# Scores moved into the gate, two expert tiles behind the output products, a projection in 32-column tiles, and part of the reads' additions on ScalarE and GpSimd

## The chip, the cores and the metric

One core of a Trainium2 chip. The metric is the device time of one execution in microseconds (us); lower is better. A core has a matrix engine (TensorE, "PE" in the profile; "PEld" is its loading of weights), VectorE (DVE), ScalarE (ACT), GpSimd (POOL) and SyncE (SP, which here only issues DMAs). Each runs its own instructions in order and waits for others through semaphores. SBUF is the on-chip memory, PSUM the accumulators that TensorE writes.

## The reference, cut to what matters

A batch of 64 signals is cut into 157 frames of 512 samples (L = 157, D = 512). All numbers are fp32.

```python
h = dct(frames)                                   # 64 x 157 x 512
x = layernorm(h)
key, query = exp(i*pi*tanh(x @ Wk)), exp(i*pi*tanh(x @ Wq))   # 4 sets x 8 planes
V = x @ Wv + bv
total = sum over sets of weight * Re(cumsum(key * V) * conj(query))
pos   = the same with fixed position phases
g = sigmoid(x @ Wg + bg)
h = h + (g * total + (1 - g) * sigmoid(pw) * pos) / norm @ Wo + bo
y = layernorm(h)
e = argmax(softmax(mean_t(y) @ Wg2 + bg2))        # one of 16 experts for each signal
h = h + score_e * (y @ We[e] + be[e])
```

The causal sums are computed as attention: a matrix of scores between frames, masked, times V (the "reads").

## The kernel before, in words

The 64 signals go through in 16 groups of four (`GB`, `NG`). A group's 4 x 160 padded frames make five tiles of 128 rows, `n` = 0 to 3 and `TAIL`; 512 columns make four blocks `c` of 128. Groups overlap: while group g is in its attention, the experts of group g-1 and the embedding (the transform) of group g+1 are worked in between. For the middle groups the order is written out by hand, and each engine's queue follows the order of these calls:

- `project_and_values(g)` (L1085): `project` (L593) makes key and query phases, then the value products (seven products of a fast block scheme, `product`, L437, matmuls at L445), with the routing of group g-1 in between, which ends in fetching its four experts' weights.
- `gate(g)` (L1133): seven products (`gate_product`, L647, matmuls L655) in the order 1, 6, 2, 7, 5, 4, 3. Products 2, 4 and 3 accumulate onto the PSUM buffers of 1, 7 and 5, which stay held until then. VectorE adds each up into `gT`, ScalarE applies the tanh (L672). Between them lie embedding tiles of group g+1 (`embed`, L259, matmuls L270 and L272; their statistics on VectorE, L232) and `fold_twice` (L125) on VectorE, which prepares the next frames. Only in the last group (`not ahead`) does `scores` stand here, behind product 5.
- `experts_and_embedding(g)` (L1151): `scores(g)` (L674, 20 matmuls at L681, then two VectorE operations that make `att`), then expert tiles TAIL, 0 and 1 of group g-1 (`expert`, L960: 16 matmuls at L940, one addition on VectorE at L951, four or eight output DMAs on SyncE), and the scaling of the next residuals on ScalarE (`embed_res`, L319, L323).
- `attention(g)` (L1177): five bias additions on GpSimd (`add_bo`, L325, L327); four reads (`read`, L685, matmuls L697), with expert tile 2 behind the second; seven output products (L710, L445) with the tail's product (L250) behind the first; expert tile 3; GpSimd's sums for the next values (`value_sums`, L411, L414).

TensorE's 128 x 128 array is used in several tile shapes, which the profile prints as rows*columns: 128*128 for most products, 128*32 for scores and experts (four signals side by side in 32 columns each), 32*128 for the reads (four signals in 32 rows each), 128*64 for the projection.

PSUM is four buffers of two banks (`psum`, L91), taken in turn: a buffer is written again when all who read its last content are done. A read takes two buffers. Its result is used by VectorE, in four operations of 128 x 320 (L705): for each buffer it multiplies the gate by the first half of the result and then adds the second half, both out of PSUM.

The functions that the change touches, with the line numbers of the profile:

Of the kernel before, what the change touches and what calls it, by code (L numbers as in the profile page):

```python
# [14 lines left out]
F32 = mybir.dt.float32  # L15
I32 = mybir.dt.int32
AF = mybir.ActivationFunctionType
ALU = mybir.AluOpType
# [4 lines left out]
P = 128  # L23
# [4 lines left out]
LP = 160  # L28
Q = P // GB
NM = LP // Q  # L30
TAIL = NM - 1
SLOT = [0, 1, 3, 4, 2]
HT = P // 2
HN = HT + 2 * P
# [3 lines left out]
F = SETS * PLANES  # L38
# [15 lines left out]
def audio_tower(ctx: ExitStack, tc: tile.TileContext, a, out):  # L54
# [21 lines left out]
    nc = tc.nc  # L76
# [4 lines left out]
    p2 = pool("p2", 2)  # L81
# [9 lines left out]
    def psum():  # L91

        return ps_mm.tile([P, 2, 512], F32, tag="mm", name="mm")

    def bank():
        return psum()[:, 0, :]
# [3 lines left out]
    add = lambda *x: nc.vector.tensor_tensor(*x, ALU.add)  # L100

    def half(x, m):
        return x[:, :, HN * m : HN * (m + 1)]
# [73 lines left out]
    wkq = const.tile([P, C, 2 * F], F32, name="wkq", tag="wkq")  # L177
# [147 lines left out]
    def add_bo(g, n):  # L325
        r = S[g]["res"][n]
        nc.gpsimd.tensor_tensor(r, r, bo, ALU.add)  # L327
# [265 lines left out]
    def project(g):  # L593


        s = S[g]
        ps = psum()[:, 0, :]
        for c in range(C):
            for k in range(2):
                nc.tensor.matmul(  # L600
                    ps[2 * F * k : 2 * F * (k + 1), :HN],
                    wkq[:, c, :],
                    half(s["xT"], k)[:, c],
                    start=(c == 0),
                    stop=(c == C - 1),
                )
        s["u"] = u = p2.tile([P, 2, HN], F32, tag="even", name="u")
        nc.scalar.activation(u[:, 0], ps[:, :HN], AF.Tanh, bias=bkq)
# [65 lines left out]
    def scores(g):  # L674

        ps = bank()
        for n in range(NM):
            lo, hi = SEES[n]
            for i in range(GB):
                to = ps[Q * i : Q * (i + 1), START[n] : START[n] + hi - lo]  # L680
                nc.tensor.matmul(to, kf[:, SLOT[n], i], qf[:, lo // Q : hi // Q, i], start=True, stop=True)  # L681
        nc.vector.tensor_tensor(att[:, 0], ps[:, :NS], hmask, ALU.mult)
        nc.vector.tensor_tensor(att[:, 1], att[:, 0], share, ALU.add)

    def read(g, c):  # L685

        s = S[g]
        parts = [psum(), psum()]
        banks = [ps[:, b, : 2 * LP] for ps in parts for b in range(2)]

        for n in (3, 0, 1, 2, TAIL):
            for i in range(GB):
                q = slice(Q * i, Q * (i + 1))
                lo, hi = SEES[n]
                to = banks[i].rearrange("p (s t) -> p s t", s=2)[:, :, lo:hi]
                by = att[q, :, START[n] : START[n] + hi - lo]
                nc.tensor.matmul(  # L697
                    to, s["v", n][q, c * P : (c + 1) * P], by, start=(n == 3), stop=(n == TAIL)
                )
        for k, ps in enumerate(parts):  # L700
            of = slice(2 * k, 2 * k + 2)
            r = ps[:, :, : 2 * LP].rearrange("p b (s n t) -> p b s n t", s=2, n=NM)
            th = s["gT"][:, c].rearrange("p (n b t) -> p b n t", n=NM, b=GB)[:, of]
            for n, op in enumerate((ALU.mult, ALU.add)):
                nc.vector.tensor_tensor(th, r[:, :, n], th, op)  # L705

    def output_product(g, i):

# [152 lines left out]
    t = lambda name, shape, dt=F32: p2.tile(shape, dt, tag=name, name=name)  # L861
# [40 lines left out]
    def pick_gate(g):  # L902

        s = S[g]
        logit, top, rev = (s.pop(k) for k in ("logit", "top", "rev"))
        nc.vector.tensor_tensor(logit, logit, over(top), ALU.subtract)
        nc.scalar.activation(logit, logit, AF.Exp)
        expf = t("expf", [P, 1])
        for i in range(GB):
            q = slice(Q * i, Q * (i + 1))  # L910
            nc.vector.tensor_scalar(expf[q], rev[q, i : i + 1], -1.0, float(E), ALU.mult, ALU.add)
        s["expi"] = expi = t("expi", [P, 1], I32)
        nc.vector.tensor_copy(expi, expf)
        den = t("den", [P, 1])
        for i in range(GB):
            q = slice(Q * i, Q * (i + 1))
            nc.vector.tensor_reduce(den[q], logit[q, i], AX.X, ALU.add)
        s["gate"] = gate = t("gate", [P, 1])
        nc.vector.reciprocal(gate, den)
# [16 lines left out]
    def expert_chunk(g, n, c, ps):  # L936

        s = S[g]
        for i in range(GB):
            nc.tensor.matmul(  # L940
                ps[Q * i : Q * (i + 1), :],
                s["x2T"][:, c, i, Q * n : Q * (n + 1)],
                s["ws"][i][:, c, :],
                start=(c == 0),
                stop=(c == C - 1),
            )

    def expert_out(g, n, ps):
        s = S[g]
        o, at = s["res"][n], Q * BLOCK[n]  # L950
        nc.vector.scalar_tensor_tensor(o, ps, s["gate"], o, ALU.mult, ALU.add)  # L951
        for i in range(GB):

            for lo, hi in ((0, Q),) if n < TAIL else ((0, Q // 2), (Q // 2, LT)):
                queue = nc.sync if g + 1 < NG or i % 2 == 0 else nc.scalar
                if g + 2 == NG and n in ORDER[1:4]:
                    queue = nc.gpsimd
                queue.dma_start(out=out[GB * g + i, at + lo : at + hi, :], in_=o[Q * i + lo : Q * i + hi, :])

    def expert(g, n, between=lambda c: None):  # L960
        ps = psum()
        for c in range(C):
            between(c)
            expert_chunk(g, n, c, ps[:, 0, :])
        between(C)
        expert_out(g, n, ps[:, 0, :])
# [166 lines left out]
    def gate(g):  # L1133
        ahead = g + 1 < NG
        for i in (1, 6, 2, 7, 5, 4, 3):
            gate_product(g, i)
            if i == 1:
                pick_gate(g - 1)
                bias(g - 1)
                fold_once(g + 1, 1)  # L1140
                add_bv(g, 0, slice(H, D))
                add_bv(g, 1)
            if i == 5:
                if not ahead:
                    scores(g)
                fold_twice(g + 1, 1)
            for n in {6: (0,), 2: (1,), 3: (2, 3, TAIL)}.get(i, ()) if ahead else ():
                embed(g + 1, n)
                embed_statistics(g + 1, n)

    def experts_and_embedding(g):  # L1151

        new = g + 1
        scores(g)
        embed_deviations(new)
        add_bias(g - 1, TAIL)
        add_bias(g - 1, 0)
        expert(g - 1, TAIL)
        load_half(g + 2, 0)
        load_half(g + 2, 1)  # L1160
        for n in (1, 2, 3):
            add_bias(g - 1, n)
        for n in range(NM):
            embed_res(new, n)
        expert(g - 1, 0)
        keep_deviations(new)
        expert(g - 1, 1)
        spread_deviations(new)
# [8 lines left out]
    def attention(g):  # L1177
        ahead = g + 1 < NG
        if ahead and g > 0:
            for n in range(NM):  # L1180
                add_bo(g + 1, n)
        if g == 0:
            for _ in weight_sums(wg, t_g, nc.gpsimd):
                pass
        for c in range(C):
            read(g, c)
            if c == 1 and ahead and g > 0:
                expert(g - 1, 2)
        S[g]["blocks"] = halves(S[g]["gT"])
        made = token_sums(g, tail=False)  # L1190
        if g == 0:
            for n in (0, 1):
                add_bo(1, n)
        for i in (1, 2, 6, 7, 5, 4, 3):
            output_product(g, i)
            if i == 1:
                for _ in range(4 if g else 3):
                    next(made)
                if g == 0:
                    scale_all(1)  # L1200
                output_tail(g)
                statistics2(g, (TAIL,))
            elif i == 6:
                normal2(g, TAIL)
            elif i == 7 and g == 0:
                next(made)
            elif i == 5 and g == 0:
                value_sums(1)
            elif i == 5 and ahead:
                scale_all(g + 1)  # L1210
        if 0 < g and ahead:
            expert(g - 1, 3)
        for of in ((0, 1),) if ahead else ((0,), (1,)):
            statistics2(g, of)
        if 0 < g and ahead:
            value_sums(g + 1)
        normal2(g, 2)
        normal2(g, 3)
        if not ahead:
            normal2(g, 0)  # L1220
# [15 lines left out]
    g = NG - 1  # L1236
# [158 lines left out]
```

## Time and profile before

| | |
|---|---|
| time, median of 3 runs | 1320.94 us (1320.14 to 1323.14) |
| profiled execution, its own time | 1321.05 us |
| its span in the trace | 1319.1 us |
| granted TensorE clock | 0.999 |
| TensorE busy in L940 (experts, 2400 records) | 276.2 us |
| TensorE busy in L697 (reads, 2048 + 512 records) | 114.6 + 23.9 us |
| TensorE busy in L600 (projection, 256 records) | 38.0 us |
| TensorE busy in L681 (scores, 640 records) | 16.6 us |
| VectorE in L705 (additions of the reads, 256) | 116.8 us, 488 ns each |
| GpSimd in L327 (bias additions, 80) | 95.1 + 20.3 us |

A line of a group in the profile reads: line, engine, operation, output<-inputs, shapes, count, busy time and mean length of one. The ends of matmuls are modelled and overlap the next, so times on TensorE are best taken from one start to the next. A timeline is a list in order of time; equal neighbours are merged, and what stands in brackets is the idle time ahead of an instruction and who ended it.

### The profile page before, as it was taken

What the parts mean: (1) busy time and instruction counts of PE and PEld (TensorE: products, weight loads), DVE (VectorE), ACT (ScalarE), POOL (GpSimd) and SP (SyncE); (2) the same over time, 40 slices, a digit from 0 to 9 for tenths busy, and PEclk for the clock granted to TensorE, in tenths of its full rate; (3) what the DMA queues carried; (4) which work ended last, traced back from release to release, by engine and by line L of the source; (5) the groups of instructions that cost most, each with busy time, mean ns of one, the idle gap of its engine ahead of it and who ended that gap; (6) DMA issues with size and microseconds to landing.
All of it is one profiled execution on the core that took longest, in us unless ns stands there. A gap on an engine that the chain in (4) does not pass through costs nothing.

```text
span 1319.1 us, 25336 instructions
## 1 busy us (share of the span) xinstructions
PE 1312.0 (99%) x9784; PEld 921.5 (70%) x9784; DVE 1065.2 (81%) x2116; ACT 405.8 (31%) x708; POOL 551.0 (42%) x706
## 2 busy tenths in 40 slices
PE   9999999999999999999999999999999999999998
PEld 6677677677676767677676766776767676776762
DVE  6888798788878878788887978888788787887683
ACT  2524233141422314234141331414233042341310
POOL 2356345243533426245153452436334262452424
PEclk9999999999999999999999999999999999999999
DMA  7015224152331425314252241523314252141506
GB/s 238 1 51 176 83 56 182 37 176 83 113 135 42 161 81 175 92 49 152 75 176 83 68 171 36 176 82 121 126 51 156 79 184 83 48 152 35 178 8 207
DMA packets 60574, 144.40 MB, mean 109 GB/s; under 512 B 14136, under 2 KB 31432, under 8 KB 52520
## 3 DMA queue, kind: packets, MB, share of 16 engines
q1 hardware_dynamic: 45620, 62.68, 16.8%
q0 software_dynamic: 14336, 79.47, 16.3%
q8 instruction: 78, 1.28, 0.4%
q10 hardware_dynamic: 500, 0.64, 0.2%
q14 instruction: 40, 0.33, 0.1%
HBM read 102.47 MB, written 20.62 MB: 93 GB/s over the span
## 4 chain that ended last, share of the span: by engine, by line
PE 97%; issue 1%; DMA 1%; POOL 1%; DVE 0%; POOLq 0%
PE mm L445 29%; PE mm L940 20%; PE mm L655 17%; PE mm L250 9%; PE mm L697 9%; PE mm L600 3%; PE mm L270 3%; PE mm L272 3%; PE mm L636 1%; PE mm L681 1%; PE mm L201 1%; DMA t_v<-in_we,rows 1%; PE mm L219 0%; PE mm L191 0%; PE mm L835 0%
## 5 line engine op out<-in xcount | busy, mean ns | idle before, releaser
L940 PE MATMUL mm<-we,x2T 128*32 128x512 f32 x2400 | 276.2, 593 | 0.0
L940 PEld LDWEIGHTS mm<-we,x2T 128*32 128x32 f32 x2400 | 130.2, 109 | 111.0 <-issue 65.2
L237 POOL TENSOR_SCALAR rstd<-mv 128x2 f32<-128x2 f32 (+1 forms) x50 | 11.7, 235 | 396.9 <-DVE mv L233 396.9
L705 DVE TENSOR_TENSOR gT<-mm,gT 128x320 f32<-128x320 f32 x256 | 116.8, 488 | 37.7 <-PE mm L697 33.1
L697 PEld LDWEIGHTS mm<-att,v 32*128 32x128 f32 x2048 | 94.9, 185 | 34.0 <-issue 21.0
L697 PE MATMUL mm<-att,v 32*128 32x320 f32 (+3 forms) x2048 | 114.6, 358 | 0.0
L327 POOL TENSOR_TENSOR res<-res,bo 128x512 f32<-128x512 f32 x64 | 95.1, 1514 | 13.1 <-ACT res L323 13.0
L771 ACT ACTIVATE x<-res,shift,rstd 128x512 f32<-128x512 f32 x61 | 46.4, 808 | 162.2 <-POOL shift L244 161.4
L232 DVE BATCH_NORM_STATS2 st<-res 128x6 f32<-128x512 f32 x128 | 87.7, 685 | 2.8
L445 PE MATMUL mm<-t_o,sum 128*128 128x256 f32 x384 | 85.5, 379 | 0.0
L951 DVE SCALAR_TENSOR_TENSOR res<-mm,gate,res 128x512 f32<-128x512 f32 x64 | 47.9, 748 | 44.9 <-PE mm L940 42.9
L515 POOL TENSOR_TENSOR v<-v,bv 128x512 f32<-128x512 f32 (+1 forms) x45 | 72.7, 1634 | 26.6 <-ACT v L464 26.6
L237 POOL TENSOR_SCALAR dev<-mv 128x5 f32<-128x5 f32 (+1 forms) x20 | 4.9, 244 | 183.2 <-DVE mv L233 182.6
L445 PE MATMUL mm<-t_v,sum 128*128 128x256 f32 x360 | 80.1, 379 | 0.0
L445 PEld LDWEIGHTS mm<-t_o,sum 128*128 128x128 f32 x384 | 73.0, 190 | 9.9
L672 ACT ACTIVATE gT<-gT,hbg 128x320 f32<-128x320 f32 x90 | 45.6, 554 | 96.4 <-DVE gT L100 96.4
L445 PEld LDWEIGHTS mm<-t_v,sum 128*128 128x128 f32 x360 | 68.4, 190 | 9.3
L894 POOL DMA_INDIRECT we<-in_we,rows x60 | 60.3, 1005 | 34.4 <-DVE rows L890 20.3
L323 ACT ACTIVATE res<-res,shift,more 128x512 f32<-128x512 f32 x64 | 46.9, 803 | 89.2 <-POOL more L313 89.2
L716 ACT COPY u<-mm 128x512 f32<-128x512 f32 x16 | 9.4, 585 | 202.9 <-PE mm L445 202.9
L250 PE MATMUL mm<-wv,xT 128*128 128x512 f32 x160 | 71.8, 592 | 0.0
L655 PE MATMUL mm<-xT,wg 128*128 128x320 f32 x240 | 69.5, 432 | 0.0
(218 smaller groups left out, 2834.5 us busy)
## 6 DMA issues: line engine op xcount, KB each, us to landing
xT<-in_frames SPq DMA_DIRECT2D x32, 640.0 KB
out<-res SPq DMA_DIRECT2D x236, 64.0 KB
x2T<-turned SPq DMA_DIRECT2D x150, 80.0 KB
x2T<-turned POOLq DMA_DIRECT2D x90, 80.0 KB
scale<-row SPq DMA_DIRECT2D x15, 320.0 KB
out<-res_t SPq DMA_DIRECT2D x62, 32.0 KB
out<-res_t SPq DMA_DIRECT2D x62, 26.0 KB
wg<-in_wg SPq DMA_DIRECT2D x1, 1024.0 KB
```

The costliest lines, as they stand in the source:

```text
L232: nc.vector.bn_stats(st, h)
L250: nc.tensor.matmul(ps, tile_of(x[:, c], n), w[:, c, :], start=(c == 0), stop=(c == C - 1))
L323: nc.scalar.activation(s["res"][n], s["res"][n], AF.Identity, bias=shift, scale=more)
L327: nc.gpsimd.tensor_tensor(r, r, bo, ALU.add)
L445: nc.tensor.matmul(ps[:, b, :], lhs[:, c, P * b : P * (b + 1)], w[:, c, :], start=(first and c == 0), stop=(c == 1), skip_group_check=not ...
L515: nc.gpsimd.tensor_tensor(v, v, by, ALU.add)
L655: nc.tensor.matmul(ps[:, o, :HN], w[:, c, o * P : (o + 1) * P], rhs[:, c], start=(first and c == 0), stop=(c == 1), skip_group_check=not f ...
L697: nc.tensor.matmul(to, s["v", n][q, c * P : (c + 1) * P], by, start=(n == 3), stop=(n == TAIL))
L705: nc.vector.tensor_tensor(th, r[:, :, n], th, op)
L894: nc.gpsimd.indirect_dma_start(out=ws[b][:, n * k : n * (k + 1)], out_offset=None, in_=of, in_offset=bass.IndirectOffsetOnAxis(ap=rows[:, ...
L940: nc.tensor.matmul(ps[Q * i : Q * (i + 1), :], s["x2T"][:, c, i, Q * n : Q * (n + 1)], s["ws"][i][:, c, :], start=(c == 0), stop=(c == C - 1),
L951: nc.vector.scalar_tensor_tensor(o, ps, s["gate"], o, ALU.mult, ALU.add)
```

## The change

- `project`: for each of the four blocks and each half of the frames, one matmul of 64 columns (keys and queries together) becomes two of 32 columns, into the same PSUM rows.
- `scores(g)` is called in `gate`, behind product 5, for every group, and no longer at the start of `experts_and_embedding`.
- `attention`: expert tile 2 moves from behind the second read to behind the output products, in front of tile 3. Two bias additions stay ahead of the reads; that of tile 2 comes behind read 0, those of tile 3 and TAIL behind read 1.
- `read`: in groups 1 to 15, for blocks 0 and 1, the second half is copied out of PSUM by ScalarE into a buffer `rest` (of two), and GpSimd adds it to the gate; VectorE only multiplies. Blocks 2 and 3 stay as they were.

```diff
         for c in range(C):
-            for k in range(2):
+            for k, n in np.ndindex(2, 2):
                 nc.tensor.matmul(
-                    ps[2 * F * k : 2 * F * (k + 1), :HN],
-                    wkq[:, c, :],
+                    ps[2 * F * k + F * n : 2 * F * k + F * (n + 1), :HN],
+                    wkq[:, c, F * n : F * (n + 1)],
                     half(s["xT"], k)[:, c],
...
-            for n, op in enumerate((ALU.mult, ALU.add)):
-                nc.vector.tensor_tensor(th, r[:, :, n], th, op)
+            nc.vector.tensor_tensor(th, r[:, :, 0], th, ALU.mult)
+            if g > 0 and c in (0, 1):
+                rest = p2.tile([P, 2, LP], F32, tag="u", name="rest").rearrange("p b (n t) -> p b n t", n=NM)
+                nc.scalar.copy(rest, r[:, :, 1])
+                nc.gpsimd.tensor_tensor(th, th, rest, ALU.add)
+            else:
+                add(th, r[:, :, 1], th)
...
             if i == 5:
-                if not ahead:
-                    scores(g)
+                scores(g)
                 fold_twice(g + 1, 1)
...
         new = g + 1
-        scores(g)
         embed_deviations(new)
...
         if ahead and g > 0:
-            for n in range(NM):
+            for n in (0, 1):
                 add_bo(g + 1, n)
...
             read(g, c)
-            if c == 1 and ahead and g > 0:
-                expert(g - 1, 2)
+            if ahead and g > 0:
+                for n in ((2,), (3, TAIL), (), ())[c]:
+                    add_bo(g + 1, n)
...
         if 0 < g and ahead:
+            expert(g - 1, 2)
             expert(g - 1, 3)
```

## The prediction

> **What bounds the kernel now.** I read the page first: its busy shares and the chain of work that ended last.
>
> ```profile
> PE 1312.0 (99%) x9784; PEld 921.5 (70%) x9784; DVE 1065.2 (81%) x2116; ACT 405.8 (31%) x708; POOL 551.0 (42%) x706
> ...
> PE 97%; issue 1%; DMA 1%; POOL 1%; DVE 0%; POOLq 0%
> ```
>
> TensorE is busy from end to end, so other engines matter only if they stop it. What remains is time lost *inside* its busy time, and for that I took its timeline through one middle group (group 3; the groups repeat every 79.95 us). Columns: start, length, line, shape, number of records (a matmul of the source leaves two).
>
> ```profile
> 285.69 2.32 PE L655 MATMUL mm<-xT,t_g 128*128 128x320 f32 x8
> 287.85 2.32 PE L655 MATMUL mm<-sum,wg 128*128 128x320 f32 x8
> ...
> 291.79 0.61 PE L270 MATMUL mm<-dct_e,xT 128*128 128x128 f32 x4
> 292.23 0.61 PE L272 MATMUL mm<-trig_o,xT 128*128 128x129 f32 x4
> 292.77 1.03 PE L681 MATMUL mm<-qf,kf 128*32 128x128 f32 x40
> 293.66 11.16 PE L940 MATMUL mm<-we,x2T 128*32 128x512 f32 x96
> 304.75 1.80 PE L697 MATMUL mm<-att,v 32*128 32x320 f32 x32
> ...
> 308.39 3.64 PE L940 MATMUL mm<-we,x2T 128*32 128x512 f32 x32
> 311.96 1.80 PE L697 MATMUL mm<-att,v 32*128 32x320 f32 x32
> ...
> 315.60 1.99 PE L445 MATMUL mm<-wo,gT 128*128 128x256 f32 x8
> 317.43 3.60 PE L250 MATMUL mm<-wo,gT 128*128 128x512 f32 x8
> ```
>
> Lengths overlap, so time is taken from start to start. One expert tile alone (L940, 308.39 to 311.96) takes 3.57; eight full records of the same 512 columns (L250, 317.43 to the next start at 320.87) take 3.44. So four 32-column tiles do run side by side, and 0.13 is lost at the two seams where the tile shape changes. But three expert tiles in a row, straight behind the scores (293.66 to 304.75), take 11.09 and not 3 x 3.44 + 0.13 = 10.45: **0.64 us is lost there, in every middle group** (11.09 to 11.16 in all fourteen). The semaphore instructions of L940 in the two stretches point to the cause:
>
> ```profile
> L940 PEldq EVENT_SEMAPHORE  x12: 51/51/51, 293.2 to 298.0; - x12
> ```
> ```profile
> L940 PEldq EVENT_SEMAPHORE  x1: 51/51/51, 307.8 to 307.8; - x1
> ```
>
> The three tiles carry 12 waits, the single tile one, and the first ten of the 12 begin at 293.23, only 0.43 before the first expert matmul, and run 0.105 apart: four ahead of the first column tile's weights, two ahead of each other's. They come due as the matmuls should start, so the four column tiles start 0.23 apart (3 x 0.23 = 0.69) and stay staggered to the end. The 40 short score matmuls leave TensorE's queue little time to run ahead; before the projection a wait of L600 passes 2.67 before its matmul.
>
> The last view is the last group, which has its scores inside the gate and four reads in a row already:
>
> ```profile
> 1243.58 1.03 PE L681 MATMUL mm<-qf,kf 128*32 128x128 f32 x40
> 1244.54 2.42 PE L655 MATMUL mm<-xT,t_g 128*128 128x320 f32 x8
> 1246.80 2.32 PE L655 MATMUL mm<-sum,wg 128*128 128x320 f32 x8
> ...
> 1252.58 2.03 PE L697 MATMUL mm<-att,v 32*128 32x320 f32 x26
> ```
>
> **The change, part by part** (us; groups 1 to 14 unless said).
>
> *Scores into the gate.* Now: 292.77 to 304.75 = 11.98 for scores and three experts. After: the scores cost 0.96 (1243.58 to 1244.54), the seam into them 0.09 (the last embedding half takes 0.54, its like 0.45; that seam stays, now into the experts), and the seam out 0.10 (the product behind them 2.26, against 2.16 in the middle): 1.15. The experts then stand behind the embedding, whose 24 records of 0.11 give the queue 2 us to run ahead (its wait for the last embedding tile passes at 289.48, 2.3 before use), and ten waits need 10 x 0.105 = 1.05. I take the experts at 10.45: 1.15 + 10.45 = 11.60, **-0.38**. If the stagger stays it is 1.15 + 11.09 = 12.24, **+0.26**.
>
> The Trainium skill, "TensorEngine Tiling (Array Packing)", Key Properties, says that a change of tiling mode drains TensorE, while tiles of one mode run independently. The seams agree: 0.09 to 0.13. By that rule alone the scores stand best where they are, next to experts of their own shape, and moving them only adds two drains; the +0.26 is that result. The row of 11.09 speaks for the other.
>
> On VectorE the two operations that make att (0.63 + 0.66, now at 297.43) come in front of the folding at 286.70. The folding then ends at 290.05 instead of 288.6, product 4 is added by 290.9, product 3 by 292.2; the embedding tiles that take their PSUM buffers start at 292.06 and 292.95. Nothing, by 0.7; if that cover goes, each 0.1 beyond it costs 1.4 in all. VectorE's embedding statistics end 1.2 later, but without att behind them, so the bias additions start as before.
>
> *Third expert tile out of the reads.* Now four reads and one expert: 304.75 to 315.60 = 10.85. Two reads without the seam out take 3.53 (71.53 to 75.06, first group), two without the seam in 3.64 - 0.05 = 3.59: 7.12. The expert joined to the fourth is 3.44 more. 10.56, **-0.29**. Its VectorE addition (L951, 0.75) and four output DMAs move along. SyncE is idle there from 317.2 to 335.8. VectorE waits for the tile's end with the statistics of tiles 0 and 1 queued behind it; they already wait for the fourth tile, whose distance to the projection is unchanged. The scale for the next xT is issued at 314.99, DMA traffic ends by 319, and its reader (L363, 328.58) comes 3.4 earlier: cover of 6.
>
> *Projection in 32-column tiles.* Expert and projection now: 331.32 to 337.19 = 5.87. After: same shape as the expert, so no seam between them: 3.44 + 0.03 (seam in) + eight rounds of 320 columns at 2.16 (285.69 to 287.85) + 0.10 (seam out) = 5.73, **-0.14** (groups 2 to 15). Twice as many instructions: the weight loads (110 ns, four overlapping, 54 ns apart by L940's 130.2 us for 2400) need 0.22 per round of 0.27. Bounds: -0.25 (no seam out either) to 0.
>
> *Additions of the reads.* Without relief, four reads in a row are limited by VectorE: in the last group the second pair takes 1252.58 to 1256.94 = 4.36 against 3.59, a loss of 0.77. With reads 0 and 1 relieved, VectorE has two multiplications (0.47 apart) per read there, ScalarE a copy of 320 columns (0.43, between 0.27 for 129 and 0.585 for 512), and ScalarE has nothing else from 304.07 to 317.6. Counted from the first read: read 0 ends at 2.0, its second multiplication and copy by 3.0, the buffers are wanted at 3.5; read 1 the same by 4.9, wanted at 5.3. So **0**, and -0.77 once in group 15.
>
> GpSimd is the narrow place. The first output product needs the halves of reads 0 and 1, its second weight load at 7.12 + 0.43 - 0.19 = 7.36. GpSimd has no addition of this shape in the trace; contiguous ones take 0.45 for 128 columns, 1.27 for 512, 1.54 for 640, so 320 should be 0.87; bounds 0.69 (512's time per column, less half its start-up) and 1.29 (0.87 x 1.88/1.27, the slowest bias addition over the usual). In order: two additions from 2.6 (1.74), the bias addition of tile 2 (1.27), two more (1.74): done at 7.35. **0**, with no margin; each 0.1 in one addition costs 0.4 a group, 5.6 in all. I take 0.87 because the bias additions at 304.86 to 308.6 run beside the same multiplications (L705) at 1.27; the slow ones (1.88, 1.72) stand beside L934, which reads two SBUF operands. The other two bias additions follow at 7.4 to 9.9; GpSimd now idles 14.2 before its next work there.
>
> The Trainium skill, "GPSIMD Engine Reference", Engine selection, advises VectorE for elementwise work, GpSimd being some 2x slower with two inputs. By that an addition is 2 x 0.488 (L705) = 0.98, the product starts 0.43 late, and the sum is 6 us worse. The rows (1.27 for 512) speak for 0.87.
>
> **Sum.** 14 x (-0.38 - 0.29 - 0.14) = -11.3, and -0.77: -12.1. The profiled execution took 1321.05 (span 1319.1), 0.1 from the median of 1320.94, so **1309.0**.
>
> **Rivals.**
> 1. *GpSimd ends late and TensorE waits at the first output product.* Slower from 0.86 a group, that is from 1.09 an addition. At 1.29: 4 x 0.42 = 1.7 x 14 = 23.5, so 1332.5; with the bias addition slow too, 1341. For: no margin, strided operands. Against: the 1.27 beside L705. 0.11. A smaller lateness (up to 0.7) gives 1312 to 1318.5: 0.12.
> 2. *The stagger stays*, or waits are the same behind the embedding: 14 x (0.26 - 0.29 - 0.14) - 0.8 = -3.2: 1318.0. For: the ten waits are still there, behind an embedding tile that itself waits for a buffer. Against: 2 us of running ahead. 0.09. (The Trainium skill's drain rule, cited above from "TensorEngine Tiling (Array Packing)", gives the same time.)
> 3. *The relief does not reach the reads* (ScalarE's copies wait for their two buffers, which GpSimd's additions free): 0.77 x 15 = 11.5 lost: 1320.5. Against: 0.4 of margin. 0.06.
> 4. The forecast: 0.62, 1306 to 1312.
>
> 0.2% (2.6 us) is about what a measurement of this kernel can tell. Faster: 0.62 + 0.12 + over half of rival 2 = 0.80; slower 0.11; within 0.2%, the rest: 0.09. The range is 1306 (projection at -0.25, and some) to 1318.5, leaving out rivals 1 in full and 3.
>
> **What would show it.** The experts behind the embedding take 10.45 from start to read, with the waits of L940 earlier than the last embedding tile; four reads take 7.1 and the next L445 starts without idle; the GpSimd additions show 0.87; L600 shows 128*32, starting 6.9 after the third expert tile. If L445 behind the reads waits for GpSimd, or L940 still takes 11.09 for three, the forecast is wrong by that row.

## The result, and the profile after

The changed kernel takes 1311.06 us (median of 4 runs, 1311.03 to 1312.64) against 1320.97 (1320.14 to 1323.14): a ratio of 0.9928, 95% interval 0.9916 to 0.9939, so 0.7% faster. The forecast was 1309.0, in a range of 1306.0 to 1318.5. The profiled execution took 1311.08, its span 1309.1.

TensorE's timeline of the changed kernel in the same group 3 (start, length, line, shape, records), from the moved scores to the first output product; new line numbers: the experts are L945, their additions L956, the routing's matmul L840:

```profile
284.40 1.03 PE L681 MATMUL mm<-qf,kf 128*32 128x128 f32 x40
285.36 2.42 PE L655 MATMUL mm<-xT,t_g 128*128 128x320 f32 x8
...
292.55 10.51 PE L945 MATMUL mm<-we,x2T 128*32 128x512 f32 x96
302.98 1.80 PE L697 MATMUL mm<-att,v 32*128 32x320 f32 x32
...
310.11 2.08 PE L445 MATMUL mm<-wo,gT 128*128 128x256 f32 x8
312.03 3.60 PE L250 MATMUL mm<-wo,gT 128*128 128x512 f32 x8
```

Three experts from start to read: 302.98 - 292.55 = 10.43, where they took 11.09. The four reads: 310.11 - 302.98 = 7.13. Both are the forecast's (10.45 and 7.12). The scores cost 0.96, and 0.10 in the product behind them (285.36 to 287.62 = 2.26 instead of 2.16), as in the last group before. The waits of the experts are still there, but early: the first at 290.46, 2.1 before the first expert matmul, and nine of the eleven have passed by 291.5.

```profile
L945 PEldq EVENT_SEMAPHORE  x11: 51/51/51, 290.5 to 296.9; - x11
```

The next stretch, from the two joined expert tiles to the value products:

```profile
246.56 7.08 PE L945 MATMUL mm<-we,x2T 128*32 128x512 f32 x64
253.45 2.34 PE L600 MATMUL mm<-xT,wkq 128*32 128x320 f32 x32
255.72 1.99 PE L445 MATMUL mm<-wv,xT 128*128 128x256 f32 x8
...
269.62 0.33 PE L840 MATMUL mm<-own,mean 128*128 128x64 f32 x2
269.92 1.99 PE L445 MATMUL mm<-wv,sum 128*128 128x256 f32 x8
```

Two experts and the projection take 255.72 - 246.56 = 9.16 (forecast 3.44 + 5.73 = 9.17). But two places have become longer. From L840 to value product 3 it is 0.30, where it was 0.17. The kernel before, in the same group (L835 is there the routing's matmul; of product 3 the view shows three records):

```profile
271.14 0.33 PE L835 MATMUL mm<-own,mean 128*128 128x64 f32 x2
271.31 0.92 PE L445 MATMUL mm<-wv,sum 128*128 128x256 f32 x3
```

And the first output product takes 1.92 up to the tail's product (310.11 to 312.03), where it took 1.83. With 0.13 and 0.09 lost, a middle group takes 79.36 from projection to projection instead of 79.95; the fourteen distances together are 8.6 shorter. The last group's four reads take 7.19 instead of 7.89, less the 0.1 behind L840: 0.6. That is 9.2 of the 10.0 by which the span fell. Of the rest some 0.6 lies in the last experts, where TensorE waits for weights from DMA, and 0.1 ahead of the first projection; neither was followed.

The 0.09 has a plain releaser (an instruction that the waiting one needed) in the list of waits (total us, times, longest), and GpSimd's timeline shows when it ended:

```profile
PEld mm L445 <- POOL gT L708: 3.2, 14, 0.2
```
```profile
306.02 1.69 POOL L708 TENSOR_TENSOR gT<-gT,rest 128x320 f32<-128x320 f32 x2 [1.42 <-ACT rest L707]
307.65 1.28 POOL L327 TENSOR_TENSOR res<-res,bo 128x512 f32<-128x512 f32 x1
308.88 1.70 POOL L708 TENSOR_TENSOR gT<-gT,rest 128x320 f32<-128x320 f32 x2
```

The last of GpSimd's additions ends at 310.58, 7.60 after the first read; the forecast had 7.35.

The 0.13 shows no releaser by name. VectorE's timeline gives one by time:

```profile
253.70 0.75 DVE L956 SCALAR_TENSOR_TENSOR res<-mm,gate,res 128x512 f32<-128x512 f32 x1 [2.68 <-PE mm L945]
...
259.69 1.88 DVE L99 TENSOR_TENSOR sum<-sum,xT 128x640 f32<-128x640 f32 x1 [1.44 <-POOL sum L411]
...
269.05 0.81 DVE L99 TENSOR_TENSOR sum<-xT,sum 128x640 f32<-128x640 f32 x1
```

The last row writes the sum that value product 3 loads as weights. It ends at 269.86, and the load starts at 269.92. Read backwards: VectorE has no gap of note from 259.69 on; there it had waited 1.44 for GpSimd's first sums (L411), which stand in GpSimd's queue behind the statistics of tiles 0 and 1, which follow the addition of the *fourth expert tile* (253.70). In the kernel before the same sum ended at 270.44 + 0.82 = 271.26, and product 3 started at 271.31: no wait shows, but no time to spare either. So my theory was: from the end of that tile two ways lead to product 3, TensorE's (projection and six products) and this one, and the shorter projection has only made TensorE wait for the other. The rival: the projection's gain is real, and the time went elsewhere.

### The profile page after: what moved, and what is told of

The parts are those of the page before. It is cut to its first block, busy times and chain, and to the rows that moved or that the text cites. A ratio compares the mean times of both kernels' runs of the same rounds, so it can differ in the third digit from the quotient of the medians.

```text
span 1309.1 us, 25859 instructions
## 1 busy us (share of the span) xinstructions
PE 1302.9 (100%) x10040; PEld 863.6 (66%) x10040; DVE 1026.9 (78%) x2056; ACT 432.5 (33%) x768; POOL 603.1 (46%) x766
## 4 chain that ended last, share of the span: by engine, by line
PE 98%; POOL 1%; DMA 1%; issue 0%; DVE 0%; POOLq 0%
PE mm L445 29%; PE mm L945 20%; PE mm L655 18%; PE mm L250 9%; PE mm L697 9%; PE mm L270 3%; PE mm L272 3%; PE mm L600 3%; PE mm L636 1%; PE mm L681 1%; PE mm L201 1%; DMA t_v<-in_we,rows 1%; PE mm L219 0%; PE mm L191 0%; PE mm L840 0%
## 5 line engine op out<-in xcount | busy, mean ns | idle before, releaser
L945 PE MATMUL mm<-we,x2T 128*32 128x512 f32 x2400 | 264.1, 593 | 0.0
L945 PEld LDWEIGHTS mm<-we,x2T 128*32 128x32 f32 x2400 | 74.8, 110 | 167.3 <-issue 165.5
L956 DVE SCALAR_TENSOR_TENSOR res<-mm,gate,res 128x512 f32<-128x512 f32 x64 | 47.9, 749 | 73.1 <-PE mm L945 73.1
L237 POOL TENSOR_SCALAR dev<-mv 128x5 f32<-128x5 f32 (+1 forms) x20 | 10.5, 525 | 196.8 <-DVE mv L233 196.2
L704 DVE TENSOR_TENSOR gT<-mm,gT 128x320 f32<-128x320 f32 x128 | 59.5, 484 | 42.6 <-PE mm L697 42.5
L100 DVE TENSOR_TENSOR gT<-mm,gT 128x320 f32<-128x320 f32 (+3 forms) x128 | 71.4, 567 | 23.9 <-PE mm L655 20.9
L327 POOL TENSOR_TENSOR res<-res,bo 128x512 f32<-128x512 f32 x64 | 81.6, 1288 | 13.1 <-ACT res L323 13.0
L445 PE MATMUL mm<-t_o,sum 128*128 128x256 f32 x384 | 85.5, 379 | 0.0
L445 PE MATMUL mm<-t_v,sum 128*128 128x256 f32 x360 | 80.1, 379 | 0.0
L445 PEld LDWEIGHTS mm<-t_o,sum 128*128 128x128 f32 x384 | 73.0, 190 | 9.9
L445 PEld LDWEIGHTS mm<-t_v,sum 128*128 128x128 f32 x360 | 68.4, 190 | 9.3
```

Of the source, the lines that this page charges most:

```text
L445: nc.tensor.matmul(ps[:, b, :], lhs[:, c, P * b : P * (b + 1)], w[:, c, :], start=(first and c == 0), stop=(c == 1), skip_group_check=not ...
L704: nc.vector.tensor_tensor(th, r[:, :, 0], th, ALU.mult)
L945: nc.tensor.matmul(ps[Q * i : Q * (i + 1), :], s["x2T"][:, c, i, Q * n : Q * (n + 1)], s["ws"][i][:, c, :], start=(c == 0), stop=(c == C - 1),
```

## The experiments

All edits are to the changed kernel, unless said. The kernel before ran beside each set: 1320.8 to 1321.4.

**The projection back in 64 columns.**

```diff
-            for k, n in np.ndindex(2, 2):
+            for k in range(2):
                 nc.tensor.matmul(
-                    ps[2 * F * k + F * n : 2 * F * k + F * (n + 1), :HN],
-                    wkq[:, c, F * n : F * (n + 1)],
+                    ps[2 * F * k : 2 * F * (k + 1), :HN],
+                    wkq[:, c, :],
```

> The changed kernel with the projection back in 64-column tiles, all else kept. Theory A: the shorter projection (0.14 us a group) only brings TensorE sooner to value product 3, which waits for VectorE's sum (L99), a chain that starts at the end of the fourth expert tile and not at the projection. Then the time stays at 1311.1 (1310.6 to 1311.6), and the first weight load behind L840 comes 0.16 after the one before it again, not 0.30. Rival B: the projection's gain is real and the 2 us between forecast and result were lost elsewhere: 14 x 0.14 = 2.0 slower, 1313.1.

Measured 1310.54 (1310.24 to 1312.35): the same time. A middle group takes 79.35, to 0.01 what it took. The stretch behind L840, in the same group, is back at 0.17:

```profile
269.58 0.33 PE L840 MATMUL mm<-own,mean 128*128 128x64 f32 x2
269.75 1.98 PE L445 MATMUL mm<-wv,sum 128*128 128x256 f32 x8
```

Theory A holds, in that the 32-column projection, as built, is worth nothing; that the other way to product 3 is the reason is tried below, where that way is made shorter.

**The scores back at the head of the experts** (`scores(g)` again in `experts_and_embedding`).

> The changed kernel with the scores back at the head of the experts, all else kept. Theory A (the experts' waits come due behind 40 short matmuls, the four column tiles start staggered): the three experts take 11.09 again from start to read, 14 x 0.38 = 5.3 slower: 1316.4. Rival B (only the drains at a change of tile shape count; two fewer here): 14 x 0.26 = 3.6 faster: 1307.4, experts at 10.45.

Measured 1316.37 (1315.57 to 1318.85), 5.3 slower, as theory A had it. Scores, experts and the read:

```profile
292.26 1.04 PE L681 MATMUL mm<-qf,kf 128*32 128x128 f32 x40
293.15 11.16 PE L945 MATMUL mm<-we,x2T 128*32 128x512 f32 x96
304.25 1.04 PE L697 MATMUL mm<-att,v 32*128 32x320 f32 x12
```

11.10 for the three experts again. Two changes of tile shape fewer, and slower: the changes of shape are the smaller effect.

**No relief in the reads** (`if False` in place of `if g > 0 and c in (0, 1)`).

> The changed kernel with VectorE doing all additions of the reads in every group. Theory A: four reads in a row are then limited by VectorE as in the last group of the kernel before, 0.77 a group over 15 groups, less the 0.09 that the first output product now waits for GpSimd in 14 of them: 11.6 - 1.3 = 10.3 slower, 1321.4. Rival B: VectorE's lateness is hidden in the middle groups (the buffers are free earlier there): within 2 of 1311.1.

Measured 1319.92 (1318.96 to 1322.15), 8.9 slower. A middle group takes 79.96, 0.60 more. The four reads take 0.69 more (304.07 to 311.89 is 7.82), nearly all of it in the second pair (4.29 from 307.60 on, the first pair 3.53), and the 0.09 goes. The mechanism is A's; its size is the 0.69 of this pair and not 0.77. Without the relief the change would be worth almost nothing (ratio to before 0.9993, interval 0.9984 to 1.0003).

**The bias addition of tile 2 behind the reads' additions.**

```diff
-                for n in ((2,), (3, TAIL), (), ())[c]:
+                for n in ((), (2, 3, TAIL), (), ())[c]:
```

> The changed kernel with the bias addition of tile 2 on GpSimd moved from between the additions of reads 0 and 1 to behind them. Theory A: the first output product waits 0.09 a group for GpSimd's last addition; it now ends 1.2 earlier, so the wait goes: 14 x 0.09 = 1.3 faster, 1309.8. Rival B: what TensorE gains there it waits for later, at value product 3, as with the projection: 1311.1. By theory A that wait hangs on the end of the fourth expert tile, which comes earlier too, so the gain stays.

Measured 1309.13 (1308.29 to 1309.6). A middle group takes 79.27, 0.09 less, so 1.3 is explained; the wait of L445 for L708 is gone from the list. The other 0.6 lies outside the middle groups (0.4 of it behind the last projection) and was not followed.

**Early waits, scores at the head of the experts.** This tells a stagger made by waits from one made by a missing drain. On top of the scores moved back, in `scores`:

```diff
         ps = bank()
+        if 0 < g < NG - 1:
+            old = S[g - 1]
+            for i in range(GB):
+                nc.tensor.matmul(
+                    ps[Q * i : Q * (i + 1), NS : NS + 1],
+                    old["x2T"][:, 0, i, Q * TAIL : Q * (TAIL + 1)],
+                    old["ws"][i][:, 0, :1],
+                    start=True,
+                    stop=True,
+                )
```

> The kernel with the scores back at the head of the experts (1316.4), and ahead of the scores four added matmuls of one column, one for each signal, that read the moved x2T and the fetched weights of the experts into unused columns of the scores' PSUM bank; the order of shapes and the drains stay. Theory A (the stagger comes from ten waits that come due as the experts should start): the waits now stand ahead of the scores, the three experts fall from 11.09 to 10.4, and the added matmuls cost 0.1 to 0.2 a group: 14 x 0.5 = 7 faster than 1316.4, 1309.5. Rival B (tiles that follow others of their own shape start staggered because nothing drains in between): experts stay at 11.09, 1318.

Measured 1306.36 (1306.1 to 1308.99), 10.0 below the same kernel without these lines. In order: the added matmuls, scores, experts, read; then the waits of the added matmuls and of the experts in that stretch:

```profile
290.42 0.24 PE L680 MATMUL mm<-we,x2T 128*32 128x1 f32 x8
290.51 1.01 PE L691 MATMUL mm<-qf,kf 128*32 128x128 f32 x40
291.34 10.49 PE L955 MATMUL mm<-we,x2T 128*32 128x512 f32 x96
301.75 1.80 PE L707 MATMUL mm<-att,v 32*128 32x320 f32 x32
```
```profile
L680 PEldq EVENT_SEMAPHORE  x9: 51/51/51, 288.3 to 289.3; - x9
```
```profile
L955 PEldq EVENT_SEMAPHORE  x3: 51/51/51, 291.1 to 295.7; - x3
```

Nine waits have moved ahead of the scores, into the time in which the embedding keeps TensorE busy. The order of the shapes is as before, and the experts take 10.41. What the waits ask for was there in time, since here they pass 2 us before the experts need them and do not hold up TensorE: it is their passing just when the experts should start that cost the time. So the stagger is a matter of waits, and theory A holds. Its size was too small: the experts gain 0.69 (11.10 to 10.41), the four matmuls cost only 0.09, and the scores shrink by 0.06 too (0.83 instead of 0.89), which makes 14 x 0.66 = 9.2 of the 10.0; the rest is less than the spread of the runs.

**GpSimd's sums ahead of the third and fourth tile.** `value_sums(g + 1)` stands ahead of `expert(g - 1, 2)` instead of behind the statistics; the second kernel has the 64-column projection as well.

> The changed kernel with GpSimd's first sums for the next values (L411, L414) issued ahead of the third and fourth expert tile, no longer behind the statistics of tiles 0 and 1. Theory A: VectorE's sums then stop waiting 1.4 for them, VectorE's chain to value product 3 is earlier, TensorE's wait of 0.135 behind L840 goes: 14 x 0.135 = 1.9 faster, 1309.2. Rival B: VectorE's chain is set by its own work or by the transposes that wait for the later statistics: no change, 1311.1, or slower.

> The same with the projection back in 64 columns. Theory A: with VectorE's chain out of the way the projection's seam counts, 0.14 a group: 2.0 slower than the run with the sums early and 32 columns, 1311.2. Rival B: the seam never counted: the same as that run.

Measured 1309.12 (1307.67 to 1310.52) and 1310.75 (1310.51 to 1311.5). The wait for L411 is gone from VectorE, and product 3 follows L840 after 0.17 again (VectorE and TensorE, first of the two kernels):

```profile
257.93 0.78 DVE L99 TENSOR_TENSOR sum<-sum,xT 128x640 f32<-128x640 f32 x1
```
```profile
269.37 0.33 PE L840 MATMUL mm<-own,mean 128*128 128x64 f32 x2
269.54 1.95 PE L445 MATMUL mm<-wv,sum 128*128 128x256 f32 x8
```

A middle group takes 79.16 with 32 columns and 79.32 with 64. So the narrow projection is worth 0.16 a group, but only once the other way to product 3 is shorter: this shows the cause. The gain over the changed kernel is 0.19 a group and not the 0.135 that theory A counted. The other 0.05 is in product 3 itself, which takes 1.78 up to the gate's first product instead of 1.83 (1.82 in the kernel before); why was not followed. That the median fell by just the 1.9 of the forecast is in part chance, as the runs of this kernel spread over 2.9.

**The third tile back in the reads** (`expert(g - 1, 2)` behind the second read).

> The changed kernel with the third expert tile back behind the second read, all else kept (the relief of reads 0 and 1 too). Theory A: two changes of tile shape come back, 0.29 a group, 4.1 slower; the first output product comes 3.4 later and no longer waits for GpSimd, 1.3 faster; the wait behind L840 stays, as it hangs on the fourth tile's end: 1311.1 + 2.8 = 1313.9. Rival B: the seams are worth nothing on the whole, as the projection's was: 1309.8 to 1311.1.

Measured 1313.57 (1312.54 to 1315.94). A middle group takes 79.56, 0.20 more: the reads and the third tile take 10.85 together again, as before the change, which is 0.28 more than 7.13 + 3.44; the 0.09 at the first output product goes, and the wait behind L840 stays (0.31). Theory A holds.

**The early waits alone, in the kernel before.**

> The kernel before, with nothing of the change, and the four one-column matmuls that read the experts' inputs ahead of the scores. Theory A: the stagger alone is worth 0.65 a group as in the run with early waits, 14 x 0.65 = 9.1 faster than 1320.9: 1311.8, about as fast as the whole change. Rival B: without the change another wait takes it back (VectorE's chain to value product 3, as with the projection): between 1313 and 1320. By theory A that chain hangs on the fourth expert tile, behind the gain, and takes nothing.

Measured 1311.08 (1310.15 to 1312.87). Four matmuls of one column reach the time of the whole change: the three experts take 10.42 (292.13 to 302.55), and a middle group 79.30 instead of 79.95. Nothing takes it back, so rival B falls.

**All together**: the bias addition later, the sums early, the scores at the experts behind the early waits.

> The changed kernel with all three: the bias addition of tile 2 behind the reads' additions, the sums early, and the scores at the head of the experts behind the four one-column matmuls. If the terms are independent: 1311.1 - 1.3 (or the 1.9 that was measured) - 1.9 - 1.6 = 1306.0. If they draw on the same cover, between 1306 and 1309.

Measured 1303.41 (1303.22 to 1305.83), ratio to before 0.9872 (0.9855 to 0.9888). A middle group takes 78.81. This is 2.6 below the forecast, and outside the range that the expectation gave. It took 1.6 for the scores and waits from a forecast of 1309.5 for that kernel, which came out at 1306.36, and 1.9 for the sums. By what a middle group measured in each run the terms add up: against the changed kernel 0.09 for the bias addition, 0.19 for the sums (79.35 to 79.16) and 0.26 for the scores and waits (79.35 to 79.09) make 0.54, and 79.35 - 0.54 = 78.81; 14 x 0.54 = 7.6, and 1311.06 - 7.6 = 1303.5. So the three do not draw on the same cover.

## Why the prediction was right, and where it was not

The direction and the main terms were right, since they were read from stretches of the same kernel that already had the shape of the change.

- *Scores, -0.38 a group.* Right, and for the reason given: 1.15 + 10.43 measured against 1.15 + 10.45. Undoing it cost 5.3, as 14 x 0.38 says. The rival by the drains alone (1318.0) fell.
- *Third tile, -0.29.* Right: 7.13 for four reads; undoing it costs 0.28 a group, less the 0.09 at the first output product.
- *Relief, 0 for four reads, and the last group.* Right in the middle groups (7.13, against 7.82 without the relief), so the rival by which it does not reach the reads (1320.5) fell; the last group gained 0.70 and not 0.77.
- *GpSimd's addition, 0.87.* The size was right (0.866, mean of 60). The Trainium skill, "GPSIMD Engine Reference", Engine selection, gave some 2x VectorE's time; it is 0.866 / 0.484 = 1.8 here, against VectorE's multiplication of the same 320 columns, one of whose inputs lies in PSUM. The relief of which these additions are a part was still worth 8.9 us. The end of the additions was 0.25 later than worked out. Failed step: "read 0 ends at 2.0, its second multiplication and copy by 3.0". The copies do not start with the multiplications but after them: the list of waits has ScalarE's copy waiting for VectorE's L704 30 times, the first copy in group 3 starts at 305.51 and not at 305.0 (the multiplication runs from 304.99 to 305.48). Why the copy has to wait for a multiplication whose result it does not use was not tried. The first addition starts 3.0 after the first read, not 2.6. The forecast named this place as having no margin, and said that it would be wrong in this row if L445 behind the reads waited for GpSimd, as it does. The first rival came true in a form smaller than its smallest price: 0.09 a group, 1.3 in all.
- *Projection, -0.14.* Wrong in what it is worth: 5.73 became true to 0.01, but not a gain. Failed step: "same shape as the expert, so no seam between them [...] -0.14". A piece of TensorE's work was shortened without asking which other chain starts at the same point and joins TensorE again. The forecast followed that chain for the moved tile, but only as far as the projection ("whose distance to the projection is unchanged"). In the kernel before, the chain ended 0.05 ahead of product 3; with the sums early the 0.16 a group came.

That the time came so near to 1309.0 is in part luck. The wait behind L840 (14 x 0.135 = 1.9) and the one for GpSimd (1.3) alone would have made 1312.2. About 1.0 that the forecast did not have, some 0.6 of it in the last experts, where TensorE waits for DMA, brought it back to 1311.06.

The Trainium skill, "TensorEngine Tiling (Array Packing)", Key Properties, says that a change of tiling mode drains TensorE. The seams agree: 0.09 to 0.16 came and went as shapes were put apart and together. It was no guide to the sign here, since the kernel with two changes of shape fewer in a group was the slower one.

## What to carry to other kernels

An engine that is busy at 99% can still lose time inside its busy time: compare the same work in two places of the same trace (three tiles in 11.09, one in 3.57), and where they differ, count the waits and how long ahead of their use they pass. Here ten waits cost 0.66 behind forty matmuls that follow each other every 0.02 us, and nothing behind 24 that take 0.11 each. Where work cannot be moved, touch its inputs once, cheaply and early. And before a shortened step on the critical engine is counted as a gain, look for the next place where that engine joins another's chain that began ahead of the step: if the chain ends just in time, the gain is given back there.

## What the runs showed of the hardware that I had not expected

- Waits in TensorE's queue follow each other about 0.105 us apart, though the profile shows 0.05 for each; ten of them ahead of four column tiles started these 0.23 apart, and they never closed up over the 24 matmuls of each (the last four start at 303.53, 303.76, 304.00 and 304.23; 11.09 against 10.43).
- A matmul of one column is cheap in column tiles: four of them (eight records) took 0.09 in all, from the first start to that of the scores.
- GpSimd's addition over strided runs of 32 columns took 0.866 for 320 columns, what a line through its contiguous additions of 128, 512 and 640 columns gives (0.87).
